# Mixture-of-experts FFN in a two-layer macaron block: every expert for every token, or tiles of routed rows

## The chip, the core and the metric

The kernel runs on one core of a Trainium2 chip. The metric is the device time of one execution in microseconds. Three runs of the kernel before gave 2809.14, 2815.56 and 2818.88 us.

## The reference

The input is 16 sequences of 256 tokens with 128 features, 4096 tokens in fp32. There are two layers; each is half an FFN, an attention, and half an FFN. Cut to what matters:

```python
x = x + 0.5 * ffn0(layernorm(x)); x = x + attn0(layernorm(x)); x = x + 0.5 * ffn0(layernorm(x))
x = x + 0.5 * ffn1(layernorm(x)); x = x + attn1(layernorm(x)); x = x + 0.5 * ffn1(layernorm(x))

# layer 0: one shared expert, eight routed ones, the two best by gate count; hidden width 128
probs = softmax(x @ gate_w + gate_b); topk_probs, topk_idx = top_k(probs, 2)
cw    = sum(one_hot(topk_idx, 8) * topk_probs)            # zero for six experts of eight
hr    = einsum('bsd,edf->ebsf', x, rw1) + rb1             # a, b = halves of hr
out_e = einsum('ebsf,efd->ebsd', silu(a) * b, rw2) + rb2
out   = shared(x) + einsum('ebsd,bse->bsd', out_e, cw)
# layer 1: eight experts, hidden width 256, gelu, the two weights divided by their sum + 1e-6
```

Attention has 16 heads of 8 features, with two softmaxes per head in layer 0 and one causal softmax in layer 1. The change leaves its arithmetic alone.

## The kernel before

All 4096 tokens stay in SBUF (`xs`) as 8 blocks of 512 tokens, tokens on partitions. An item is a sublayer on one block; `items` (lines 517 to 522) lists 8 blocks of FFN00, then attention 0, FFN01, FFN10, attention 1 and FFN11 (first digit the layer, second the FFN in it). An item yields units of up to three stages, and `step` runs one stage each of three successive units side by side. In the second or third unit of an item, the next item's `prepare` is written into the instruction order. Each engine's queue takes its instructions in the order of the program.

An FFN item's `prepare` normalizes the block (`normalized_T`: statistics on VectorE, a power on GpSimd at line 142, transposes on TensorE, a copy on ScalarE) and computes the gates (`gates`: logits at 165, ranks by comparing every pair of experts at 187 to 194, weights at 195 to 207). The weights per token, `cw`, are transposed, written to DRAM (`cwD`, line 214), and read back spread over all partitions, 256 KB for each expert (`load_spread`, line 263).

Each unit is one expert (in layer 1 half an expert, as its hidden width is two times 128) on all 512 tokens: two products with 512 columns (231, 232), an activation on ScalarE (234), one VectorE instruction for bias and product (236), a GpSimd multiply by the spread weights (300) that zeroes what was not routed, and the output product added in PSUM (316). A block has 9 units in layer 0 and 16 in layer 1. After the last one, `finish_ffn` transposes the sum and adds half of it to x. All expert weights lie in SBUF from the start, loaded by DMAs from ScalarE's queue.

Attention works on two sequences per block; its units cover four heads and one softmax each. VectorE's maxima (421 in layer 0, 416 in layer 1) go to `mpad`, which TensorE transposes before the second set of scores (393, tile `ss_a`).

Of the kernel before, what the change touches and what calls it, by code (L numbers as in the profile page):

```python
# [9 lines left out]
BF = mybir.dt.bfloat16  # L10
AF = mybir.ActivationFunctionType
# [4 lines left out]
P = 128  # L16
# [5 lines left out]
def kernel(ctx: ExitStack, tc: tile.TileContext, a: dict, out: bass.AP):  # L22
    """Two macaron layers (half FFN, attention, half FFN) over x [B, T, C].

    x stays in SBUF, tokens on partitions. Each sublayer works on blocks of 512 tokens (two
    sequences). Feature-major activations [C, tokens] feed the matrix products. Everything is fp32,
    except for the causal mask's constants.
    """
# [6 lines left out]
    NCH = TB // P  # token chunks of a block  # L35
    BPB = TB // T  # sequences of a block
    NBLK = B * T // TB
    NT = T // P  # token chunks of a sequence
    G = H // 4  # heads go four to a group, each in a strip of 32 partitions
# [5 lines left out]

    const = ctx.enter_context(tc.tile_pool(name="const", bufs=1))
# [3 lines left out]
    gatep = ctx.enter_context(tc.tile_pool(name="gate", bufs=2))  # L50
    ffp = ctx.enter_context(tc.tile_pool(name="ffn", bufs=3))
    atp = ctx.enter_context(tc.tile_pool(name="attn", bufs=2))
    dram = ctx.enter_context(tc.tile_pool(name="dram", bufs=2, space=bass.MemoryType.DRAM))
# [26 lines left out]
    gate_w0 = wp.tile([P, E], FP, name="gate_w0")  # L80
    nc.scalar.dma_start(out=gate_w0, in_=a["L0_ffn_gate_w"])
    gate_b0 = bcast_row(a["L0_ffn_gate_b"], E, "gate_b0")

# [5 lines left out]
    # Layer 0: expert 0 here is the shared one, the routed ones follow.  # L89
    w1_0 = [load(a["L0_ffn_sw1"][0], [P, 2 * F0], "sw1")]  # L90
    w2_0 = [load(a["L0_ffn_sw2"][0], [P, C], "sw2")]
    for e in range(E):
        w1_0.append(load(a["L0_ffn_rw1"][e], [P, 2 * F0], f"rw1_{e}"))
        w2_0.append(load(a["L0_ffn_rw2"][e], [P, C], f"rw2_{e}"))
    # The output biases, a row per expert and the shared one's last.
    b2_0 = wp.tile([E + 1, C], FP, name="b2_0")
    nc.scalar.dma_start(out=b2_0[0:E, :], in_=a["L0_ffn_rb2"])
    nc.scalar.dma_start(out=b2_0[E : E + 1, :], in_=a["L0_ffn_sb2"])

    # Hidden biases with features on partitions: load rows, transpose.  # L100
    def hidden_bias(parts, name):
        rows = sum(p.shape[0] for p in parts)
        raw = wp.tile([rows, P], FP, name=name + "_raw")
        r = 0
        for p in parts:
            nc.scalar.dma_start(out=raw[r : r + p.shape[0], :], in_=p)
            r += p.shape[0]
        ps = small(name + "_ps")
        nc.tensor.transpose(ps[:, :rows], raw, ident[:rows, :rows])
        t = wp.tile([P, rows], FP, name=name)  # L110
        nc.vector.tensor_copy(t, ps[:, :rows])
        return t

    b1_0 = hidden_bias(
        [
            a["L0_ffn_sb1"].rearrange("e (k f) -> (e k) f", f=P),
            a["L0_ffn_rb1"].rearrange("e (k f) -> (e k) f", f=P),
        ],
        "b1_0",
    )  # L120

# [1 line left out]
    mhalf = const.tile([P, NCH], FP, name="mhalf")  # L123
    nc.gpsimd.memset(mhalf, -0.5)
    # earlier[e, f] = 1 where f < e: of equal gates, the lower index goes first.
# [7 lines left out]
    def normalized(src, nchunk, dst, key):  # L133
        """dst = (src - mean) / sqrt(var + eps) over the last axis, chunk by chunk."""
# [13 lines left out]
    def normalized_T(n, key):  # L148
        """The block's layernorm with features on partitions, [C, 512]."""
        xn = lnp.tile([P, NCH, C], FP, tag="xn", name=f"xn_{key}")  # L150
        normalized(xs[n], NCH, xn, key)
        ps = small(f"xnT_ps_{key}")
        for c in range(NCH):
            nc.tensor.transpose(ps[:, c * P : (c + 1) * P], xn[:, c, :], ident)
        xnT = lnp.tile([P, TB], FP, tag="xnT", bufs=3, name=f"xnT_{key}")
        nc.scalar.copy(xnT, ps)
        return xnT

    def gates(xnT, gate_w, gate_b, layer, key):
        """The experts' weights for the block's tokens, [E (+ 1), 512] with a row of ones for the  # L160
        shared expert: in SBUF, and in DRAM, from where rows are spread over the partitions."""
        rows = E + 1 if layer == 0 else E
        ps = small(f"lg_ps_{key}")
        for c in range(NCH):
            nc.tensor.matmul(
                ps[:, c * E : (c + 1) * E], lhsT=xnT[:, c * P : (c + 1) * P], rhs=gate_w,
                start=True, stop=True,
            )
        lg = gatep.tile([P, NCH, E], FP, tag="lg", name=f"lg_{key}")
        nc.vector.tensor_tensor(  # L170
            lg, ps[:, : NCH * E].rearrange("p (c e) -> p c e", e=E),
            gate_b.unsqueeze(1).to_broadcast([P, NCH, E]), ALU.add,
        )
        mx = gatep.tile([P, NCH, 1], FP, tag="mx", name=f"mx_{key}")
        nc.vector.tensor_reduce(mx, lg, AX.X, ALU.max)
        ex = gatep.tile([P, NCH, E], FP, tag="ex", name=f"ex_{key}")
        nc.vector.tensor_tensor(ex, lg, mx.to_broadcast([P, NCH, E]), ALU.subtract)
        nc.scalar.activation(ex, ex, AF.Exp)
        sm = gatep.tile([P, NCH, 1], FP, tag="sm", name=f"sm_{key}")
        nc.vector.tensor_reduce(sm, ex, AX.X, ALU.add)  # L180
        nc.vector.reciprocal(sm, sm)
        # rank = how many experts go before this one; the first two are taken.
        other = lg.unsqueeze(2).to_broadcast([P, NCH, E, E])
        own = lg.unsqueeze(3).to_broadcast([P, NCH, E, E])
        gt = gatep.tile([P, NCH, E, E], FP, tag="gt", name=f"gt_{key}")
        eq = gatep.tile([P, NCH, E, E], FP, tag="eq", name=f"eq_{key}")
        nc.vector.tensor_tensor(gt, other, own, ALU.is_gt)
        nc.vector.tensor_tensor(eq, other, own, ALU.is_equal)
        nc.gpsimd.tensor_tensor(
            eq, eq, earlier.unsqueeze(1).to_broadcast([P, NCH, E, E]), ALU.mult  # L190
        )
        nc.vector.tensor_tensor(gt, gt, eq, ALU.add)
        rank = gatep.tile([P, NCH, E], FP, tag="rank", name=f"rank_{key}")
        nc.vector.tensor_reduce(rank, gt, AX.X, ALU.add)
        nc.vector.scalar_tensor_tensor(ex, rank, 1.5, ex, ALU.is_lt, ALU.mult)
        cw = gatep.tile([P, NCH, E + 1], FP, tag="cw", name=f"cw_{key}")
        nc.vector.tensor_tensor(cw[:, :, 0:E], ex, sm.to_broadcast([P, NCH, E]), ALU.mult)
        if layer == 0:
            nc.gpsimd.memset(cw[:, :, E : E + 1], 1.0)
        else:  # L200
            top = gatep.tile([P, NCH, 1], FP, tag="top", name=f"top_{key}")
            nc.vector.tensor_reduce(top, cw[:, :, 0:E], AX.X, ALU.add)
            nc.vector.tensor_scalar(top, top, 1e-6, None, ALU.add)
            nc.vector.reciprocal(top, top)
            nc.vector.tensor_tensor(
                cw[:, :, 0:E], cw[:, :, 0:E], top.to_broadcast([P, NCH, E]), ALU.mult
            )
        psT = small(f"cwT_ps_{key}")
        for c in range(NCH):
            nc.tensor.transpose(psT[:rows, c * P : (c + 1) * P], cw[:, c, 0:rows], ident)  # L210
        cwT = gatep.tile([E + 1, TB], FP, tag="cwT", bufs=3, name=f"cwT_{key}")
        nc.scalar.copy(cwT[:rows], psT[:rows])
        kept = dram.tile([E + 1, TB], FP, tag="cw", bufs=3, name=f"cwD_{key}")
        nc.sync.dma_start(out=kept[:rows], in_=cwT[:rows])
        return cwT, kept

    def finish_ffn(n, acc, key):
        """x += 0.5 * acc^T"""
        oT = ffp.tile([P, TB], FP, tag="oT", bufs=2, name=f"oT_{key}")
        nc.scalar.copy(oT, acc)  # L220
        ps = small(f"o_ps_{key}")
        for c in range(NCH):
            nc.tensor.transpose(ps[:, c * P : (c + 1) * P], oT[:, c * P : (c + 1) * P], ident)
        nc.vector.scalar_tensor_tensor(
            xs[n].rearrange("p c d -> p (c d)"), ps, 0.5, xs[n].rearrange("p c d -> p (c d)"),
            ALU.mult, ALU.add,
        )
# [17 lines left out]
    class FFN:  # L245
        def __init__(self, layer, which, n, last=False):
            self.layer, self.n, self.last = layer, n, last
            self.key = f"f{layer}{which}_{n}"
# [375 lines left out]
    while under_way:  # L624
        step()
# [33 lines left out]
```

## Time and profile before

| | us |
|---|---|
| median of three runs (lowest to highest) | 2815.56 (2809.14 to 2818.88) |
| profiled execution, its span from the first to the last instruction | 2803.8 |
| busy TensorE, VectorE, ScalarE, GpSimd in it | 2554.9, 1174.8, 1010.8, 625.8 |
| FFN00, 36 to 262 | 226 |
| attention 0, 262 to 1305 | 1043 |
| FFN01 and FFN10, 1305 to 1855 | 550 |
| attention 1, 1855 to 2440 | 585 |
| FFN11, 2440 to 2803 | 363 |

PE is TensorE's matrix products, PEld its weight loads, DVE VectorE, ACT ScalarE, POOL GpSimd, SP SyncE. Names that end in q stand for an engine's own queue. A line such as "L300 POOL TENSOR_TENSOR hw_f<-h_f,cwb_f ... x384 | 485.4, 1266 | 644.8 <-DVE h_f" gives source line, engine, operation, tile written and tiles read, count, busy time in us, the mean of one in ns, the time the engine idled before such instructions, and what ended that idling. A row of windows gives the window and its length, each engine's busy time with its count of instructions, the granted clock of TensorE as a share of full speed, the share of the DMA engines' time, and GB/s. An fp32 product has two records for each pass in the timeline ("x2").

### The profile page before, as it was taken

To read this page: it belongs to the slowest core of one execution; us is meant where nothing else is said; L and a number is where in the kernel's file an instruction comes from. 1 tells how busy PE (TensorE), PEld (TensorE's weight loads), DVE (VectorE), ACT (ScalarE), POOL (GpSimd) and SP (SyncE) were. 2 spreads that over 40 slices of the span, in tenths; PEclk is the share of its full clock that TensorE was granted. 3 is DMA by queue.
4 is the path that set the end of the run, shared out by engine and by line. 5 is a ranking of instruction groups with operands and counts; after the bars stand their busy time and mean duration, and the time that the engine had idled before them with its cause. 6 is when DMAs were issued, how large, how long until landed. Compare 5 with 4: busy or idle time off the path is not lost.

```text
span 2803.8 us, 36494 instructions
## 1 busy us (share of the span) xinstructions
PE 2554.9 (91%) x14660; PEld 1376.0 (49%) x14660; DVE 1174.8 (42%) x2553; ACT 1010.8 (36%) x1525; POOL 625.8 (22%) x595
## 2 busy tenths in 40 slices
PE   4999888888888888887999999999999999999999
PEld 2444555555555555553444444445555555544443
DVE  4443444444444444445444343434443444434332
ACT  1333434333334333344334333323333333333332
POOL 3443000000000010002444444440000000144444
PEclk8999989999989888899999999999999999999999
DMA  5221000000000000000121102110000000021110
GB/s 143 79 74 59 1 1 1 1 1 1 1 1 1 1 1 1 1 20 31 61 91 61 61 31 61 37 35 1 1 1 1 1 1 1 20 65 42 60 56 32
DMA packets 63968, 79.90 MB, mean 28 GB/s; under 512 B 16355, under 2 KB 29734, under 8 KB 63798
## 3 DMA queue, kind: packets, MB, share of 16 engines
q1 hardware_dynamic: 45856, 71.88, 7.8%
q10 hardware_dynamic: 17942, 5.69, 0.9%
q8 instruction: 115, 1.88, 0.3%
q14 instruction: 55, 0.45, 0.1%
HBM read 74.89 MB, written 2.65 MB: 28 GB/s over the span
## 4 chain that ended last, share of the span: by engine, by line
PE 79%; DVE 13%; DMA 2%; POOL 2%; issue 2%; ACT 1%; ACTq 0%; SPq 0%; POOLq 0%; DVEq 0%
PE sm_a L393 12%; PE acc_f L316 10%; PE hid_f L231 10%; PE ss_a L393 9%; PE hid_f L232 9%; PE av_a L454 8%; DVE mpad L421 6%; PE pq_a L376 3%; PE pq_a L377 3%; PE po_a L468 2%; PE pm_a L432 2%; PE ss_a L387 2%; DMA cwb_f<-cwD_f 2%; PE sm_a L387 1%; PE acc_f L309 1%
## 5 line engine op out<-in xcount | busy, mean ns | idle before, releaser
L300 POOL TENSOR_TENSOR hw_f<-h_f,cwb_f 128x512 f32<-128x512 f32 x384 | 485.4, 1266 | 644.8 <-DVE h_f L236 586.3
L441 ACT ACTIVATE ex_a<-ss_a 128x1024 f32<-128x1024 f32 (+1 forms) x384 | 365.4, 952 | 588.0 <-PE ss_a L393 587.9
L393 PE MATMUL ss_a<-q_a,k_a 32*128 32x256 f32 (+1 forms) x3072 | 426.0, 397 | 151.7 <-DVE mpad L421 146.3
L236 DVE SCALAR_TENSOR_TENSOR h_f<-hid_f,b,s_f 128x512 f32<-128x512 f32 x384 | 287.9, 750 | 572.3 <-ACT s_f L234 571.4
L234 ACT ACTIVATE s_f<-hid_f,b 128x512 f32<-128x512 f32 x384 | 263.8, 687 | 622.7 <-PE hid_f L232 622.2
L421 DVE TENSOR_REDUCE mpad<-sm_a 128x4 f32<-128x1024 f32 x256 | 313.6, 1225 | 403.5 <-PE sm_a L393 307.0
L393 PE MATMUL sm_a<-k_a,q_a 32*128 32x256 f32 (+1 forms) x3072 | 429.5, 398 | 0.5 <-ACT k_a L379 0.5
L393 PEld LDWEIGHTS ss_a<-q_a,k_a 32*128 32x128 f32 x3072 | 272.2, 192 | 264.4 <-DVE mpad L421 198.8
L393 PEld LDWEIGHTS sm_a<-k_a,q_a 32*128 32x128 f32 x3072 | 253.7, 193 | 142.7 <-issue 90.7
L454 PE MATMUL av_a<-ex_a,vaug 128*32 128x256 f32 (+1 forms) x3072 | 266.8, 385 | 0.0
L316 PE MATMUL acc_f<-hw_f,W 128*128 128x512 f32 x512 | 263.1, 596 | 1.3 <-POOL hw_f L300 1.3
L232 PE MATMUL hid_f<-xnT_f,W 128*128 128x512 f32 x512 | 262.8, 595 | 0.0
L231 PE MATMUL hid_f<-xnT_f,W 128*128 128x512 f32 x512 | 261.7, 593 | 0.7 <-ACT ex_a L441 0.7
L490 POOL TENSOR_TENSOR o_a<-pr_a 128x256 f32<-128x256 f32 x16 | 11.6, 724 | 876.6 <-DVE pr_a L487 876.6
L416 DVE TENSOR_REDUCE mpad<-sm_a 128x2 f32<-128x256 f32 (+1 forms) x256 | 131.0, 554 | 109.9 <-PE sm_a L393 109.3
L316 PEld LDWEIGHTS acc_f<-hw_f,W 128*128 128x128 f32 x512 | 95.7, 190 | 127.2 <-issue 123.8
L454 PEld LDWEIGHTS av_a<-ex_a,vaug 128*32 128x32 f32 x3072 | 96.7, 112 | 116.1 <-issue 58.3
L231 PEld LDWEIGHTS hid_f<-xnT_f,W 128*128 128x128 f32 x512 | 95.8, 190 | 114.4 <-issue 107.1
L232 PEld LDWEIGHTS hid_f<-xnT_f,W 128*128 128x128 f32 x512 | 94.0, 190 | 102.2 <-issue 101.8
L464 ACT COPY avs_a<-av_a 128x512 f32<-128x512 f32 (+1 forms) x128 | 61.3, 479 | 218.4 <-PE av_a L454 218.4
L316 PE MATMUL acc_f<-hw_f,rw 128*128 128x512 f32 x256 | 132.5, 599 | 6.9 <-POOL hw_f L300 6.7
L231 PE MATMUL hid_f<-xnT_f,rw 128*128 128x512 f32 x256 | 133.1, 602 | 2.6 <-ACT ex_a L441 2.0
(132 smaller groups left out, 2464.1 us busy)
## 6 DMA issues: line engine op xcount, KB each, us to landing
cwb_f<-cwD_f SPq DMA_DIRECT2D x256, 256.0 KB
x<-in_L_attn_x_dram SPq DMA_DIRECT2D x8, 256.0 KB
W<-in_L_ffn_W_dram ACTq DMA_DIRECT2D x8, 256.0 KB
out_dram<-x SPq DMA_DIRECT2D x8, 256.0 KB
rw<-in_L_ffn_rw_dram ACTq DMA_DIRECT2D x8, 128.0 KB
W<-in_L_ffn_W_dram ACTq DMA_DIRECT2D x8, 128.0 KB
rw<-in_L_ffn_rw_dram ACTq DMA_DIRECT2D x8, 64.0 KB
cwD_f<-cwT_f SPq DMA_DIRECT2D x16, 18.0 KB
```

The lines of the kernel that those rows point to most:

```text
L231: nc.tensor.matmul(hidden[:, 0, :], lhsT=lhs_act, rhs=xnT, start=True, stop=True)
L232: nc.tensor.matmul(hidden[:, 1, :], lhsT=lhs_lin, rhs=xnT, start=True, stop=True)
L234: nc.scalar.activation(s, hidden[:, 0, :], func, bias=bias_act)
L236: nc.vector.scalar_tensor_tensor(h, hidden[:, 1, :], bias_lin, s, ALU.add, ALU.mult)
L300: nc.gpsimd.tensor_tensor(hw, h, self.spread[e], ALU.mult)
L316: nc.tensor.matmul(self.acc, lhsT=w2, rhs=made["h"], start=False, stop=last)
L376: nc.tensor.matmul(pq[:, 0:T], lhsT=wq[:, w, g, :], rhs=seq["x"], start=True, stop=True)
L393: nc.tensor.matmul(sc[:, jj, col : col + size], lhsT=stationary[s, w, c * P : (c + 1) * P], rhs=moving[s, w, first : first + size], start= ...
L416: nc.vector.tensor_reduce(mp[:, c, 2 * jp : 2 * jp + 2, D : D + 1], sc[:, :, col : col + size], AX.X, ALU.max, negate=True,)
L421: nc.vector.tensor_reduce(mp[:, :, 2 * jp : 2 * jp + 2, D].rearrange("p c j -> p j c"), sc.rearrange("p j (c s) -> p j c s", s=T), AX.X, A ...
L441: nc.scalar.activation(ex[:, 2 * jp : 2 * jp + 2, :], sc[:, :, : self.cols], AF.Exp, scale=ATT_SCALE)
L454: nc.tensor.matmul(av[32 * j : 32 * j + 32, w * T + first : w * T + first + size], lhsT=seq["v"][:, c, 4 * g + j, :], rhs=u["ex"][:, j, co ...
```

## The change

The tokens are taken in halves of four blocks (2048 tokens), and each FFN computes only the rows that were routed.

- At the start the experts' weights, output bias (repeated on 128 rows) and hidden bias are copied into one DRAM table per layer (`wcat`, by `gather_weights`), and two DRAM buffers for rows (`slots_x`, 5888 rows each) are filled with zeros. All of these DMAs are issued from ScalarE's queue.
- `dispatch` normalizes four blocks, computes the gates, ranks, counts and start positions for the whole half, and so each token's two slots (`idx`), its two weights (`wgt`) and each tile's expert (`rows`). Then 32 indirect DMAs on GpSimd's queue scatter the normalized rows, 128 rows of 512 bytes each, to slots in DRAM. Each expert's rows start at a multiple of 256.
- `units` first runs, in layer 0, the shared expert on the four blocks, and then 23 tiles of 256 rows. For each tile SyncE reads the expert's row into a register, loads that expert's weights from DRAM (263 KB in layer 0, 461 KB in layer 1, four buffers) and the tile's rows. TensorE transposes the rows, computes the hidden products (two or four with 256 columns) and the output products (two or four with 128 columns), VectorE adds the output bias, and the rows are written to DRAM (`slots_y`) from ScalarE's queue.
- `combine` gathers the two rows of each token back with 32 indirect DMAs of 128 rows on GpSimd's queue; VectorE adds each, times its weight, to x.
- The order is written out by hand: `dispatch`, `combine` and the normalization for attention are generators in the list `between`, of which `advance` takes a few parts after each unit. The attention of one half is placed between FFNs of the other.
- The spread loads, the GpSimd multiply by the weights, the transposes of `cw` and of the output sum, and the weights kept in SBUF are gone.

```diff
+    def gather_weights(layer):
+        w1, w2, b2, b1 = srcs[layer]
+        wc = dram.tile([E * P, WC[layer]], FP, name=f"wcat{layer}")
+        nc.scalar.dma_start(out=wc[:, 0:col], in_=w1.rearrange("e p f -> (e p) f"))
...
+        nc.scalar.dma_start(
+            out=sx.rearrange("(p i) d -> p i d", p=P),
+            in_=zero.to_broadcast([P, NSLOT // P, C]),
+        )
...
     class FFN:
+        def dispatch(self):
...
+            nc.vector.tensor_tensor(eq, other, own, ALU.is_equal)
+            nc.gpsimd.tensor_tensor(eq, eq, earlier.unsqueeze(1).to_broadcast(s4), ALU.mult)
...
+            for c in range(HCH):
+                for j in range(2):
+                    s = nc.gpsimd.indirect_dma_start(
+                        out=self.sx[:, :],
+                        out_offset=bass.IndirectOffsetOnAxis(ap=idx[:, j, c : c + 1], axis=0),
+                        in_=self.xn[c // NCH][:, c % NCH, :], in_offset=None,
+                    )
+                yield
...
+        def load_tile(self, j):
+            wt = ffp.tile([P, WC[layer]], FP, tag="wt", bufs=4, name=f"wt_{k}")
+            row = nc.sync.value_load(self.rows[0:1, j : j + 1], min_val=0, max_val=(E - 1) * P)
+            nc.sync.dma_start(out=wt, in_=wcat[layer][bass.ds(row, P), :])
+            xg = ffp.tile([P, 2, C], FP, tag="xg", bufs=4, name=f"xg_{k}")
+            ld = nc.sync.dma_start(
+                out=xg, in_=self.sx[j * TS : (j + 1) * TS, :].rearrange("(p i) d -> p i d", i=2)
+            )
+            for s in self.scattered:
+                tc.add_manual_dep(ld.ins, s.ins.name, SYNC, reason="every row may be here")
...
+        def output(self, u):
...
+            nc.vector.tensor_tensor(
+                y, ps[:, :TS].rearrange("p (i d) -> p i d", i=2), b2, ALU.add
+            )
+            nc.scalar.dma_start(
+                out=self.sy[j * TS : (j + 1) * TS, :].rearrange("(p i) d -> p i d", i=2), in_=y
+            )
...
+        def combine(self):
+            for i, n in enumerate(self.blocks):
+                for c in range(NCH):
+                    t = i * NCH + c
+                    for j in range(2):
+                        g = ffp.tile([P, C], FP, tag="g", bufs=8, name=f"g_{self.key}_{t}_{j}")
+                        nc.gpsimd.indirect_dma_start(
+                            out=g[:, :], out_offset=None, in_=self.sy[:, :],
+                            in_offset=bass.IndirectOffsetOnAxis(
+                                ap=self.idx[:, j, t : t + 1], axis=0
+                            ),
+                        )
+                        nc.vector.scalar_tensor_tensor(
+                            xs[n][:, c, :], g, self.wgt[:, j, t : t + 1], xs[n][:, c, :],
+                            ALU.mult, ALU.add,
+                        )
+                    yield
...
+    compute(0, 0, 0, 3)
+    compute(0, 0, 1, 3)
+    attend(0, 0, 0, 4, 1)
+    attend(0, 1, 0, 2, 2)
+    compute(0, 1, 0, 2)
+    attend(0, 1, 2, 4, 2)
+    compute(1, 0, 0, 2)
+    compute(0, 1, 1, 2)
+    attend(1, 0, 0, 3, 3)
+    compute(1, 0, 1, 2)
+    attend(1, 0, 3, 4, 3)
+    attend(1, 1, 0, 4, 2)
+    compute(1, 1, 0, 3)
+    compute(1, 1, 1, 3)
```

`compute(layer, which, half, rate)` runs the units of one FFN half and `attend(layer, half, first, last, rate)` the attention of some of its blocks; `rate` is how many parts of the generators follow each unit.

## The prediction

> **What bounds the kernel now.** I read the page's first part for the busiest engine, then the table by windows, cut at the stages, then the timeline, the groups and the chain of waits for the price of one instruction. A difference of 0.3% (8.4 us) is about what a measurement of this kernel can tell from no change.
>
> ```profile
> PE 2554.9 (91%) x14660; PEld 1376.0 (49%) x14660; DVE 1174.8 (42%) x2553; ACT 1010.8 (36%) x1525; POOL 625.8 (22%) x595
> PE 79%; DVE 13%; DMA 2%; POOL 2%; issue 2%; ACT 1%; ACTq 0%; SPq 0%; POOLq 0%; DVEq 0%
> ```
> TensorE is busy 91% and carries 79% of the chain that ended last. The windows are: start, FFN00, attention 0, FFN01 with FFN10, attention 1, FFN11 (columns: length, busy time of PE, PEld, DVE, ACT, POOL; granted clock, DMA share, GB/s).
>
> ```profile
> 0.00:36.00 36.00, 8.74 (x25) 5.04 (x25) 17.61 (x83) 2.67 (x4) 15.73 (x41) 1.00 0.63 143
> 36.00:262.00 226.00, 207.12 (x570) 93.07 (x571) 91.91 (x220) 80.59 (x114) 87.89 (x82) 0.96 0.26 87
> 262.00:1305.00 1043.00, 886.24 (x7326) 545.65 (x7324) 455.05 (x741) 411.04 (x599) 70.04 (x93) 0.91 0.01 2
> 1305.00:1855.00 550.00, 530.07 (x1428) 237.19 (x1428) 241.28 (x637) 194.70 (x275) 255.32 (x220) 1.00 0.18 60
> 1855.00:2440.00 585.00, 567.31 (x4387) 336.16 (x4386) 232.65 (x592) 202.51 (x366) 27.86 (x25) 0.99 0.01 3
> 2440.00:2803.00 363.00, 355.40 (x928) 158.89 (x926) 136.36 (x283) 119.27 (x171) 168.95 (x137) 1.00 0.15 49
> ```
> The FFN stages are bound by PE (530 of 550 us): 226 + 550 + 363 = 1139 us can shrink. The two attentions, 1628 us, are not changed in their own work. The timeline of a steady FFN stretch gives the price of a product: starts 0.86 us apart for 512 fp32 columns, so 0.43 for 256.
>
> ```profile
> 1600.15 1.02 PE L316 MATMUL acc_f<-hw_f,W 128*128 128x512 f32 x2
> 1601.01 1.02 PE L231 MATMUL hid_f<-xnT_f,W 128*128 128x512 f32 x2
> 1601.87 1.02 PE L232 MATMUL hid_f<-xnT_f,W 128*128 128x512 f32 x2
> ```
> Other prices are from the groups, and the landing of a 256 KB load (4.73) and of a small write to DRAM (1.77) from the chain of waits at 1304 to 1340 us:
>
> ```profile
> L300 POOL TENSOR_TENSOR hw_f<-h_f,cwb_f 128x512 f32<-128x512 f32 x384 | 485.4, 1266 | 644.8 <-DVE h_f L236 586.3
> L236 DVE SCALAR_TENSOR_TENSOR h_f<-hid_f,b,s_f 128x512 f32<-128x512 f32 x384 | 287.9, 750 | 572.3 <-ACT s_f L234 571.4
> L435 DVE TENSOR_TENSOR q_a<-pm_a,q_a 128x256 f32<-128x256 f32 x192 | 80.1, 417 | 74.4 <-PE pm_a L432 74.4
> L379 ACT ACTIVATE k_a<-pq_a,k_ones 128x256 f32<-128x256 f32 x192 | 92.1, 480 | 0.0
> ```
> ```profile
> 1320.84 1.77 DMA cwD_f<-cwT_f
> 1324.02 4.73 DMA cwb_f<-cwD_f
> ```
>
> **What goes.** Per block, 9 units (layer 0) or 16 (layer 1) of three 512-column products: 16 blocks x 9 + 16 x 16 = 400 units, 400 x 3 x 0.86 = 1032 us of PE. With them go 384 POOL multiplies and 256 spread loads of 256 KB; both were hidden behind PE, so their going buys nothing by itself.
>
> **What comes, on PE.** Each FFN half runs 23 tiles of 256 rows whatever the routing (16 would hold 4096 chosen rows, 7 are for padding), 92 tiles per layer. A layer 0 tile: two transposes of 0.135, two 256-column products of 0.43, two 128-column ones of 0.225 = 1.58 us; layer 1: 0.27 + 4 x 0.43 + 4 x 0.225 = 2.89. That is 92 x 4.47 = 411 us, with 16 shared units of 2.62 (two 512-column, four 128-column) 453 us in all, instead of some 1100.
>
> **A tile's real period.** PE will not be the bound: the weights come from DRAM per tile into 4 buffers, and tile j+4's load can go only when tile j's last DVE instruction has read its bias. The circle for layer 0: issue 0.38 (the median of the spread load's issue), landing 4.73, hidden 0.86, ACT 0.48, DVE 0.42, output 0.45, DVE 0.42 = 7.7, and about two other tiles' PE work queued ahead, 3.2: 10.9 / 4 = 2.7 us. Layer 1: landing 5.9 (4.73 and 0.34 MB more at the 280 GB/s of the window 36:44 below), hidden 1.72, two ACT 0.96, DVE 0.42, output 0.9, DVE 0.42, issue 0.38 = 10.7, with two tiles' 5.8 16.5 / 4 = 4.1. Bytes: 525 and 723 KB a tile, at 280 GB/s 1.9 and 2.6 us, just under. Ends: 2.0 and 3.1 (bytes and PE) below; above, PE at half clock, which this trace shows where PE has idled:
>
> ```profile
> 36.00:44.00 8.00, 0.00 (x0) 0.00 (x0) 0.00 (x0) 0.00 (x0) 0.00 (x0) 0.72 0.88 280
> 44.00:52.00 8.00, 2.10 (x5) 1.03 (x5) 0.47 (x3) 2.12 (x3) 0.58 (x2) 0.50 0.69 218
> ```
> At half clock a tile's PE work is 3.2 and 5.8. I take 2.7 and 4.1, as PE would be busy 58 to 70%, nearer to attention 0 (85% busy, clock 0.91) than to a stop.
>
> **Scatters and gathers.** 32 scatters and 32 gathers of 128 rows per half, on POOL's queue, 16 phases. No indirect DMA is in the trace. Below: a plain issue of 128 rows, 0.38 us. Above: a small DRAM transfer that nothing overlaps, 1.77, or 2.3 with the next issue and a hand-over. The nearest row is a POOL instruction over all partitions, 1.27; I take 1.3, 42 us a phase. On the path: the first scatters (the first tile's load waits for all of them), the first gathers (their 32 DVE additions stand between tiles 0 and 4 of the second half, so DVE waits and later outputs behind them), the second half's gathers at the start of attention 0 (32 additions within four units, ahead of the maxima that PE waits for), and the last gathers. The other twelve lie beside tiles or attention; what they cost is in the stalls of steps 4 to 7.
>
> A rule of the Trainium skill, "DMA: Bandwidth & Descriptors", section "Anatomy of one DMA — SWDGE (gpsimd) path", fits such DMAs as 2.0 us and bytes over 436 GB/s. By it a 64 KB piece would be an estimate of 2.15 us and, if they ran one at a time, the total would come out near 2880, slower than now.
>
> DVE and POOL also get in each other's way here: the 128x32 instruction L195 takes 155 ns at best and 845 at worst.
>
> ```profile
> L195 DVE SCALAR_TENSOR_TENSOR ex_f<-rank_f,ex_f x32: 155/580/845, 32.8 to 2722.3; 128x32 f32<-128x32 f32 x32
> ```
> The Trainium skill ("SBUF — State Buffer", section "SBUF: two separate sides") speaks against this change in the same place: a DMA that GpSimd issues cannot get its descriptors written while DVE holds the port they share, and it gives 620 ns alone against 3100 beside a copy. At that price 32 pieces would be an estimate of 99 us and the change a loss; the trace before has no such DMA.
>
> **The sum by stages.**
> 1. Start. Weights copied DRAM to DRAM (2.1 and 3.7 MB, read and written), 6 MB of zeros and x: about 20 MB at 280 GB/s, 70 us; ACT's queue issues 33 of these ahead of its first copy, so its first xnT waits (PE, DVE and POOL also have waits on late loads in front). Then gates 10, routing 18 (three 1024-column DVE instructions of some 1.7, POOL's multiply 2.5, rank 1.6, about thirty of 0.2 and hand-overs), scatters 42, load 6: first tile at 146.
> 2. First half 23 x 2.7 = 62, and 10 where SP reads row numbers of the next half before loads of the fifth tile on: 218.
> 3. Second half: shared units 10.5, 62, gathers' stall 30 (42 less the four tiles beside them): 321. Before, 262.
> 4. Attention 0: 1043 + 30 (gathers in front) + 40 (two halves' routing and additions on DVE, whose maxima bound PE there already): 1434.
> 5. FFN01 and FFN10: shared 21, 46 x 2.7 = 124, 46 x 4.1 = 189, stalls 30: 1798. That is 364 against 550.
> 6. Attention 1: 585 + 55, as in 4: 2438.
> 7. FFN11: 189, stalls 30, the last 32 gathers uncovered 42, additions and output 5: 2704. That is 266 against 363.
> The sum stands against the profiled execution's span, 2803.8: 100 us less. The median of the runs lies 11.8 above that span; so 2716 us.
>
> **Rivals.**
> A. The indirect DMAs pace the kernel, 2.3 us each. One more us apiece costs 32 on each of the four exposed phases (128) and on half of four partly covered ones (64), about 190: 2906, slower. For it: DVE waits in order for each gather. Against it: the program lets eight be under way at once. It decides from 1.85 us on ((2815 - 2716) / 190 = 0.53 over 1.3).
> B. The tiles run at the half-clock ends, 3.2 and 5.8: 92 x 0.5 + 92 x 1.7 = 202 more, 2918, slower. It decides from 0.54 us more per tile. Against: a PE that becomes full gets its clock back.
> C. All is hidden: tiles 2.0 and 3.1 (92 x 1.7 = 156 less), pieces 0.8 (95 less): 2465.
> That less is computed than said cannot be: the tile count is fixed.
>
> **How the numbers follow.** The forecast, 2600 to 2807, 0.48; C 0.12; A 0.18; B 0.18; between forecast and loss, within 0.3%, 0.04. Faster 0.60, same 0.04, slower 0.36. The range takes in C's end nearly and A's and B's: 2480 to 2930; its own range for the likeliest case is 2600 to 2807.
>
> **What would show it.** The first tile's transposes near 146 us; tiles 2.7 and 4.1 us apart in compute stretches, with PE waiting on the weight's DMA; POOL's indirect DMAs 1.3 us apart; DVE waits on gathers of about 30 us at the start of the second half and in front of attention 0; 42 us of gathers after the last tile. Attention stages longer by over 100 us, or indirect DMAs over 1.85 us, would make it wrong; so would a clock near 0.5 in the tile stretches.

## The result, and the profile after

The changed kernel took 3078.07 us (median of four, 3071.83 to 3086.34), the kernel before on the same chip 2812.35: a ratio of 1.0954 (1.0925 to 1.0983). The forecast was 2716, a gain, with a range up to 2930, so its sign was wrong. The same code, run again on a later occasion (label a1_again), took 2805.77 us (median of ten, 2791.95 to 2824.06) against 2811.11, a ratio of 0.9991 (0.9966 to 1.0015). Both belong to the result: 272 us of the loss come and go with a condition of the chip that the experiments describe, and some 90 us by which the forecast was too low stay in either.

The page, busy time and shares of the chain: the first occasion, then the same code run again.

```profile
PE 2101.9 (68%) x14757; PEld 1417.9 (46%) x14757; DVE 1136.4 (37%) x2802; ACT 828.4 (27%) x1467; POOL 654.2 (21%) x706
PE 51%; DVE 12%; another core or an unknown queue 10%; issue 9%; DMA 8%; POOL 5%; ACT 2%; ACTq 1%; SPq 1%; POOLq 0%; DVEq 0%
```
```profile
PE 2084.3 (75%) x14757; PEld 1404.3 (50%) x14757; DVE 1139.3 (41%) x2802; ACT 829.2 (30%) x1467; POOL 653.4 (23%) x706
PE 53%; DVE 13%; DMA 12%; POOL 9%; issue 9%; ACT 1%; ACTq 1%; SPq 1%; POOLq 0%; DVEq 0%
```
TensorE has 2102 us of work, not 2555, and no longer bounds the kernel: it is busy 68%. "Another core or an unknown queue" holds 10% of the first chain, on a kernel with one core; in the second it is gone. Both groups of indirect DMAs cost about what was forecast, 0.95 us and 0.30 between two, so 1.26 each and 40 us for 32, which I call a train:

```profile
L534 POOL DMA_INDIRECT g_f<-slots_y,idx_f x256 | 243.0, 949 | 647.6 <-DMA slots_y<-y_f 227.8
L400 POOL DMA_INDIRECT slots_x<-xn_f,idx_f x256 | 246.5, 963 | 203.7 <-DVE high_f L381 79.4
```
What the others do meanwhile is the finding. Windows of the first occasion, undisturbed attention and then the scatter train at 1004.8 (length, PE, PEld, DVE, ACT, POOL, clock, DMA share, GB/s):

```profile
500.00:540.00 40.00, 34.48 (x308) 22.11 (x310) 15.26 (x19) 17.45 (x26) 0.00 (x0) 0.97 0.01 1
1005.00:1045.00 40.00, 7.06 (x60) 3.68 (x52) 3.14 (x5) 2.63 (x3) 30.55 (x32) 0.59 0.24 78
```
TensorE does 7 us of work in 40 instead of 34, and VectorE and ScalarE do not fill the gap. The chain in that train (start, length, what):

```profile
1009.89 2.11 PE sm_a L622 x8
1012.00 0.03 issue
1012.02 0.02 DVEq L664
1012.04 0.04 issue
1012.09 0.43 DVE q_a L664
1012.51 37.53 another core or an unknown queue
1050.05 0.02 issue
1050.07 1.24 DVE mpad L650
```
The maxima at 1050.07 wait for TensorE alone, by their semaphore; TensorE's last product before them ended at 1014.65. The timeline shows the same on ScalarE, whose copy also waits only for the product above it:

```profile
1008.22 1.67 PE L683 MATMUL av_a<-ex_a,vaug 128*32 128x256 f32 x16
...
1034.64 0.58 ACT L693 COPY avs_a<-av_a 128x512 f32<-128x512 f32 x1 [25.86 <-remote]
```
The product ended at 1009.89, the copy began 24.8 us later. The trace also records each raise of the counter (the semaphore) by which the others learn that a product has ended. The raise itself comes late: five of TensorE's products here ended at 1007.92, 1008.29, 1009.89, 1010.95 and 1014.64, the raises on record are at 1010.57, 1012.00, 1034.62, 1050.05 and 1050.14, and the copy and the maxima begin 0.02 us after the third and the fourth. Outside trains a raise comes 0.02 us after the end of its product on average; inside them about 5 us, 42.8 at worst, some 870 us over 174 raises (each end taken with the next raise on record; 31 of 2210 raises are missing from the record, so single values may be too high). The waits of the whole run that end on such a late raise ("remote") do not depend on this matching. They sum to 690 us on VectorE and ScalarE, often side by side; the kernel before and a1_again have none. The longest of them (us in total, times, longest):

```profile
ACT avs_a L693 <- remote: 142.3, 6, 38.1
DVE mpad L645 <- remote: 94.0, 6, 35.6
DVE mpad L650 <- remote: 76.8, 3, 37.6
```
I call this the hold-up. By stages, in us of span:

| | forecast | first occasion | run again | p6_both (below) |
|---|---|---|---|---|
| start and FFN00 | 321 | 392 | 348 | 343 |
| attention 0 | 1113 | 1292 | 1219 | 1116 |
| FFN01, FFN10 | 364 | 360 | 316 | 317 |
| attention 1 | 640 | 766 | 681 | 636 |
| FFN11 | 266 | 263 | 226 | 231 |
| sum | 2704 | 3073 | 2790 | 2643 |

The stages are cut at VectorE's first and last addition of the output bias (L516) in an FFN half. So what lies between attention's last product and the first finished tile, some of the shared expert's units among it, counts as attention. Cut at attention's last product on TensorE instead, the two attentions are 1245 and 734 us on the first occasion, 1172 and 649 run again, and 1084 and 617 in p6_both.

### The profile page after: what moved, and what is told of

Read it like the earlier page. It is cut to its first block, busy times and chain, and to the rows that moved or that the text cites. A ratio compares the mean times of both kernels' runs of the same rounds, so it can differ in the third digit from the quotient of the medians.

```text
span 3072.5 us, 38949 instructions
## 1 busy us (share of the span) xinstructions
PE 2101.9 (68%) x14757; PEld 1417.9 (46%) x14757; DVE 1136.4 (37%) x2802; ACT 828.4 (27%) x1467; POOL 654.2 (21%) x706
## 4 chain that ended last, share of the span: by engine, by line
PE 51%; DVE 12%; another core or an unknown queue 10%; issue 9%; DMA 8%; POOL 5%; ACT 2%; ACTq 1%; SPq 1%; POOLq 0%; DVEq 0%
PE sm_a L622 10%; PE ss_a L622 8%; PE av_a L683 7%; PE hid_f L484 6%; DVE mpad L650 5%; DMA wt_f<-wcat 5%; PE pq_a L605 3%; PE pq_a L606 3%; PE po_a L697 2%; PE pm_a L661 2%; POOL g_f L534 2%; PE ss_a L616 2%; PE y_ps_f L510 2%; DMA xg_f<-slots_x 2%
## 5 line engine op out<-in xcount | busy, mean ns | idle before, releaser
L484 PE MATMUL hid_f<-xT_f,wt_f 128*128 128x256 f32 x1104 | 309.5, 425 | 130.4 <-DMA wt_f<-wcat 71.9
L534 POOL DMA_INDIRECT g_f<-slots_y,idx_f x256 | 243.0, 949 | 647.6 <-DMA slots_y<-y_f 227.8
L484 PEld LDWEIGHTS hid_f<-xT_f,wt_f 128*128 128x128 f32 x1104 | 218.1, 210 | 185.9 <-DMA wt_f<-wcat 73.2
L400 POOL DMA_INDIRECT slots_x<-xn_f,idx_f x256 | 246.5, 963 | 203.7 <-DVE high_f L381 79.4
L492 ACT ACTIVATE s_f<-hid_f,wt_f 128x256 f32<-128x256 f32 x276 | 120.9, 471 | 385.5 <-PE hid_f L484 234.0
L497 DVE SCALAR_TENSOR_TENSOR h_f<-hid_f,wt_f,s_f 128x256 f32<-128x256 f32 x276 | 125.3, 478 | 249.7 <-ACT s_f L492 193.7
L510 PE MATMUL y_ps_f<-wt_f,h_f 128*128 128x128 f32 x1104 | 174.1, 292 | 63.5 <-ACT xT_f L473 26.6
L510 PEld LDWEIGHTS y_ps_f<-wt_f,h_f 128*128 128x128 f32 x1104 | 160.2, 205 | 82.3 <-ACT xT_f L473 27.7
L721 POOL TENSOR_TENSOR o_a<-pr_a 128x256 f32<-128x256 f32 x16 | 11.6, 722 | 860.9 <-DVE pr_a L718 860.9
L605 PE MATMUL pq_a<-xnT_a,wq 128*128 128x256 f32 x384 | 145.8, 469 | 0.0
L516 DVE TENSOR_TENSOR y_f<-y_ps_f,wt_f 128x256 f32<-128x256 f32 x184 | 75.9, 420 | 181.5 <-PE y_ps_f L510 90.5
```

The source lines that it names most:

```text
L400: s = nc.gpsimd.indirect_dma_start(out=self.sx[:, :], out_offset=bass.IndirectOffsetOnAxis(ap=idx[:, j, c : c + 1], axis=0), in_=self.xn[c ...
L484: nc.tensor.matmul(hid[:, z, k * TS : (k + 1) * TS], lhsT=wt[:, (base + k) * P : (base + k + 1) * P], rhs=xT, start=True, stop=True,)
L497: nc.vector.scalar_tensor_tensor(h[:, k, :], hid[:, 1, k * TS : (k + 1) * TS], wt[:, bias + lin0 + k : bias + lin0 + k + 1], s[:, k, :], A ...
L510: nc.tensor.matmul(ps[:, i * P : (i + 1) * P], lhsT=u["h"][:, k, i * P : (i + 1) * P], rhs=wt[:, w2 + k * C : w2 + (k + 1) * C], start=(k ...
L534: nc.gpsimd.indirect_dma_start(out=g[:, :], out_offset=None, in_=self.sy[:, :], in_offset=bass.IndirectOffsetOnAxis(ap=self.idx[:, j, t : ...
L605: nc.tensor.matmul(pq[:, 0:T], lhsT=wq[:, w, g, :], rhs=seq["x"], start=True, stop=True)
```

## The experiments

Theory 1: trains of indirect DMAs hold up TensorE's hand-overs. Theory 2: the program's own waits for gathers and staged rows cost the time. Theories 3 and 4 came later.

**Trains added to the kernel before.** Each of these adds 256 DMAs of 64 KB whose data nobody reads, meant for attention 0.

m1_train asks for eight groups of 32, m2_spread for two per unit:

```diff
+    def extra(n):
+        for _ in range(n):
+            g = ffp.tile([P, C], FP, tag="g", bufs=8, name=f"g_{turn['g']}")
+            nc.gpsimd.indirect_dma_start(out=g[:, :], out_offset=None, in_=x_rows,
+                in_offset=bass.IndirectOffsetOnAxis(ap=rowi[:, 0:1], axis=0))
...
+            if NBLK <= i < 2 * NBLK and j == 4:
+                extra(32)      # m2_spread: extra(2) in every unit
```


> The kernel before, with 8 trains of 32 indirect gathers (128 rows of x, 64 KB each) on GpSimd's queue, one train per block of attention 0; nothing reads what they bring. Theory 1 (a train of indirect DMAs holds up the other engines' semaphore updates until it ends, as the gaps of 18 to 46 us in the trace after suggest): each train freezes attention for about 30 of its 40 us, so 8 x 30 = 240 us more, about 3050, and the same gaps in the semaphore updates. Theory 2 (the time after is lost in waits of the program: DVE's additions, the tile loads and the row buffers wait for the data): nobody waits for these, so within 10 us of before.

> The same 256 unread gathers, two after each of the 128 units of attention 0 instead of in trains. GpSimd's queue has nothing else to wait for, so it may still run them in trains early; if they do come out evenly, theory 1 expects a loss in proportion to the time in which one is under way (256 x 1.26 = 320 us at the most, 100 to 250 if hand-overs slip between). Theory 2: within 10 us of before.

3011.72 and 3014.97 us (2807.76 before; 1.072 and 1.073). Nothing ties the gathers to their units, so GpSimd ran all of them ahead, from 19 to 400 us in both kernels, and FFN00's multiplies (L300) queued behind them: TensorE's products wait 126 us for them in m1_train, 7.9 in the kernel before. That is a loss by GpSimd's order, which says nothing of the theories. TensorE's raises were 0.01 us late. I passed over that then; it counts below.

m3_plain has plain DMAs of the same size from GpSimd's queue instead (0.54 us each).

> The trains of m1_train with plain DMAs of the same 64 KB from GpSimd's queue in place of indirect ones. If the hold-up belongs to any DMA that GpSimd writes descriptors for, the loss is like m1_train's per DMA; if it belongs to the indirect ones alone, it is under 20 us. Theory 2: within 10 us of before.

2863.99 us (1.0195). GpSimd ran these ahead too, from 19 to 243 us, and TensorE's products wait 28 us for the multiplies.

m4_train ties each train to a unit of attention 0 by row numbers that VectorE makes from that unit's maxima:

```diff
+        nc.vector.scalar_tensor_tensor(
+            idx, mp[:, 0, 0, D : D + 1], 0.0, rowf, ALU.mult, ALU.add)
+        for _ in range(32 if turn["u"] % 16 == 4 else 0):   # m7_pairs: range(2)
+            g = ffp.tile([P, C], FP, tag="g", bufs=8, name=f"g_{turn['g']}")   # m5_train2: 2
+            nc.gpsimd.indirect_dma_start(...)               # m6_plain: dma_start, to DRAM
```


> The kernel before with 8 trains of 32 unread indirect gathers, this time tied to attention 0: the row numbers come from a small DVE instruction in each of its 128 units (0.17 us, about 20 us in all at the most), and one unit in 16 is followed by 32 gathers with 8 buffers. In m1_train GpSimd ran all 256 ahead in FFN00, in front of its multiplies, so that run does not tell the theories apart. Theory 1 (a train holds up the hand-overs between the other engines): PE does a fifth to a half of its usual work in each 40 us train, 8 x 20 to 32 = 160 to 260 us more, 2970 to 3070. Theory 2 (program waits): at most the 20 us of small instructions, under 2830.

> m4_train with 2 buffers for the gathers in place of 8, so that at most two are under way. If what holds up the others is the number of indirect DMAs under way, the loss per train falls by half or more, to under 100 us in all; if it is GpSimd's work on each of them, it stays as in m4_train, per time spent in the train. Theory 2: under 2830.

> m4_train with plain DMAs (64 KB from SBUF to DRAM) from GpSimd's queue in place of the indirect ones, 8 trains of 32. If any DMA whose descriptors GpSimd writes holds up the others, 8 x 32 x 0.54 us = 138 us of trains cost 70 to 110 us more than before; if only indirect ones do, it is at most the 20 us of small instructions. Theory 2: the same 20 us.

> m4_train's 256 gathers as pairs, two after the maxima of each of the 128 units, instead of 8 trains. If the hold-up is of the time in which an indirect DMA is being issued, whatever its neighbours, 128 pairs of 2.5 us cost as much as the trains (160 to 260 us); if a train has to build up (its first 7 to 11 us passed freely in the trace after), pairs cost under 60 us. Theory 2: under 2830.

Against 2814.06 on the same occasion: m4_train 3095.84 (1.1008), 282 us or 35 for each train that nobody reads; m5_train2, whose two buffers put its gathers 1.37 us apart, 3010.59 (1.0705), 25 for each train, between its two expectations; m6_plain 2843.82 (1.0112); m7_pairs 2806.27 (0.9991, 0.9968 to 1.0015). The windows of m4_train, its first train and then no train, and of m7_pairs:

```profile
292.00:332.00 40.00, 11.41 (x86) 7.03 (x78) 3.16 (x5) 4.13 (x7) 30.31 (x32) 0.63 0.18 51
400.00:440.00 40.00, 33.18 (x329) 20.33 (x328) 18.13 (x27) 16.77 (x24) 0.00 (x0) 1.00 0.00 1
```
```profile
271.00:311.00 40.00, 34.01 (x283) 21.70 (x283) 17.27 (x26) 17.11 (x25) 11.60 (x12) 0.96 0.07 20
```
The same 256 gathers cost 282 us in trains and nothing in pairs, and no engine needs their data: theory 1 for this occasion, with no help from theory 2. The waits of VectorE and ScalarE that end on a late raise sum to 499 us in m4_train, 286 in m5_train2, and none in m6_plain and m7_pairs. GpSimd's order is not the reason here: VectorE waits 13.4 us for attention's own GpSimd instructions (`o_a`, L492) in m4_train, as in the kernel before.

m8_space and m9_space_s put a GpSimd memset of 128x768 or 128x256 after each gather of m4_train, which stretches 1.25 us to 1.88 and 1.44.

> m4_train with a GpSimd memset of 128x768 (about 0.75 us) between the gathers of a train, so one every 2.0 us in place of 1.25; the same 256 gathers, trains of 64 us. Theory 1 as the runs have left it (the hold-up builds up only where indirect DMAs follow one another at GpSimd's own pace; m7_pairs cost nothing): at most the 20 us of small instructions, 2800 to 2840. If the hold-up is of any time in which GpSimd works on an indirect DMA in a long row, spaced or not: 2950 to 3100.

> m8_space with a shorter memset (128x256, 0.31 us), one gather every 1.6 us. It places the threshold: m4_train at 1.25 us a gather lost 35 us per train, m5_train2 at 1.37 lost 24. If what is saturated needs about 1.4 us per DMA, next to nothing is lost here (under 2850); if it needs 1.7 or more, over 2900.

2903.23 us (1.0336), 12 for a train, and 2943.89 (1.048), 17, on another chip and occasion. In m9_space_s 140 us of the waits of VectorE and ScalarE end on a late raise; in m8_space none does. Most of what m8_space loses comes from GpSimd's order: its trains last 60 us, attention's GpSimd instructions queue behind them, and VectorE waits 76.2 us for these instead of 13.4 (TensorE in turn 75.1 us for VectorE's `q_a` instead of 5.4):

```profile
DVE st_a L138 <- POOL o_a L492: 76.2, 16, 11.0
```
So the hold-up shrinks with the gap between indirect DMAs: 499, 286 and 140 us of such waits at 1.25, 1.37 and 1.44 us, and none at 1.88.

**The changed kernel, taken apart.** p1_paced lets each scatter read a ScalarE copy of its rows in one of four buffers, and each gather's addition come two parts later, with six buffers instead of eight:

```diff
+                stage = lnp.tile([P, C], FP, tag="stage", bufs=4, name=f"stage_{key}_{c}")
+                nc.scalar.copy(stage, self.xn[c // NCH][:, c % NCH, :])
```


> The changed kernel with its 512 indirect DMAs paced: each scatter reads a copy that ScalarE makes in the unit in which it is due (4 buffers), and each gather's buffer (6) is given back by additions that come two parts later, so at most a few indirect DMAs can run in a row. Theory 1, if a hold-up ends with each short group: 150 to 300 us faster than the changed kernel, 2780 to 2920; if only the number of indirect DMAs counts, no change (3078). Theory 2: the additions wait less for their gathers, up to 120 us faster (the 118.5 us that DVE's additions waited for gathers).

2880.4 us (1.0251), 198 less than the first occasion, and raises 2.2 us late at most. I took that for a proof that waits in GpSimd's queue cure the hold-up. Its trains say otherwise: still 32 DMAs 1.26 us apart. The last three runs took this reading down.

p2_space puts the 128x768 memset after each indirect DMA except the first 32 and the last 32.

> The changed kernel with the memset of m8_space after each indirect DMA, except in the first scatters and the last gathers, which nothing runs beside. Theory 1: the freezes of 14 trains go, 14 x 25 to 32 us less, and the trains' own length (64 us) is waited for where tiles or x wait for them, 4 x 24 us back: 2700 to 2850. Theory 2 (waits for the data): the data come later, so slower than 3078 by up to 200.

2917.19 us (1.0389), 161 less than the first occasion, between the ranges of the two theories. Both are at work: late raises end 53 us of waits, all beside the first 32 scatters, which have no memset; but the other trains now last some 60 us, and VectorE waits 285 us for gathers instead of 118.5. The spacing takes the hold-up away and pays for it in the program's waits.

p4_anchor ties each pair of row numbers to the unit being written, and adds one part later:

```diff
+            nc.vector.scalar_tensor_tensor(
+                idx, anchor["col"].to_broadcast([P, 2]), 0.0, at[:, :, c], ALU.mult, ALU.add)
...
+            anchor["col"] = h[:, 0, 0:1]            # a tile's hidden rows
...
+                anchor["col"] = mp[:, 0, 0, D : D + 1]   # attention's maxima
```


> The changed kernel, with each pair of row numbers made by a small DVE instruction that reads a column of the unit being written (a hidden tile or an attention tile), so that a scatter's or gather's two indirect DMAs go out with that unit and not in a train of 32; eight gather buffers, and a gather's addition one part later. Theory 1 (a train of indirect DMAs at GpSimd's own pace holds up the hand-overs from PE to DVE and ACT until it ends; pairs of them do not, as the 256 gathers in pairs cost nothing in the kernel before): about ten of the sixteen trains go, some 25 to 35 us each, less what the anchors and the later additions cost: 2700 to 2850, most likely near 2790, PE's updates late by under 0.3 us on average inside the remaining pairs. Theory 2 (the program's own waits for gathers and staged rows cost the time, whatever the spacing): it stays at 2950 to 3080, and DVE's waits on gathers do not shrink.

p5_plain uses plain DMAs of the same size, to and from fixed rows, with a memset of 128x640 after each:

```diff
-                    s = nc.gpsimd.indirect_dma_start(
+                    s = nc.gpsimd.dma_start(
+                        out=self.sx[k * P : (k + 1) * P, :], in_=self.xn[c // NCH][:, c % NCH, :]
...
+                        s = nc.gpsimd.dma_start(out=g[:, :], in_=self.sy[k : k + P, :])
```


> The changed kernel with its 512 indirect DMAs replaced by plain DMAs of the same size from GpSimd's queue, to and from fixed rows of the same DRAM buffers, and a GpSimd memset of 128x640 after each so that they keep a pace of about 1.25 to 1.9 us: the rows are not routed, the waits of the program stay as they are. Theory 1 (the indirect kind of DMA holds up the hand-overs): without it the forecast's sum holds for the rest, 2650 to 2800, and PE's updates come under 0.1 us late. Theory 2 (the waits for 32 paced DMAs of any kind, in their order, cost the time): 2900 to 3080, as the waits are the same.

p4_anchor 2883.3 (1.0252), above the range of theory 1; p5_plain 2666.82 (0.9492), inside it, and 411 less than the first occasion, without a late raise. Not all of the 411 is due to the kind of DMA. a1_again, with indirect DMAs and no hold-up, took 2805.77, so 139 us have another reason, and p5_plain changes more than the kind: its gathers are 1.10 us apart, and its scatters read no row numbers, so they do not wait for the ranks. The first tile's transposes come at 145 us instead of 166.5, and the scatters that a1_again sends in one train at 951 go in five groups of 4 and 8 between 459 and 895. In p4_anchor the lateness follows the length of what is left of the trains: summed over the raises inside, less than 0.3 us for a group of two, 1.6 for four, 7 for eight, 63 for sixteen, on average.

So p6_both allows one pair in each unit (two in four places), and takes the next half's rows through the layer norm only after the last half's scatters; p7_nopause drops its memsets.

```diff
+        while pair["last"] == pair["tick"] and pair["n"] >= most and under_way:
+            yield WAIT
...
+                yield from next_unit(key + "s")     # and before each pair of gathers
```


> p4_anchor taken on: not more than one pair of indirect DMAs with one unit (two in four places where an FFN needs them soon), the next half's layer norm after the last one's scatters, and between tiles a GpSimd memset of 128x256 after each indirect DMA. Only the first 32 scatters and the last 32 gathers are left as trains. Theory 1 (trains hold up the hand-overs): what p4_anchor still loses against p5_plain (2883 less 2667) is mostly in its remaining trains of 4 to 32, so it should come to 2700 to 2820, and might pass the kernel before. Theory 2 (the waits of the program): 2850 to 2950, since the pairs now come later than in p4_anchor, and tiles and norms wait for them.

> p6_both without the memsets between tiles: there a pair per tile of about 2.8 us leaves GpSimd only 0.3 us between pairs. Theory 1: the hand-overs are late again in the six FFN stretches, so it is 20 to 100 us slower than p6_both. Theory 2: the same as p6_both or a little faster, as the DMAs are issued no later.

2652.92 us (0.9457, 0.9429 to 0.9485) and 2650.56 (0.9446, 0.9412 to 0.9479): faster than both kernels, by more than either theory gave. p7_nopause is a miss, as theory 1 expected 20 to 100 us more; perhaps the tie to a tile already spaces its pairs. Late raises still end 93 us of VectorE's and ScalarE's waits in p6_both, against 690 on the first occasion. p6_both's page:

```profile
PE 2075.4 (79%) x14757; PEld 1404.0 (53%) x14757; DVE 1157.9 (44%) x3050; ACT 826.1 (31%) x1465; POOL 731.7 (28%) x930
PE 52%; DVE 15%; DMA 12%; issue 9%; POOL 6%; another core or an unknown queue 2%; ACT 1%; ACTq 1%; SPq 1%; DVEq 0%; POOLq 0%
```
**Which condition.** s1_staged has only p1_paced's staged scatters, a1_again nothing new.

> The changed kernel with one half of p1_paced: each scatter reads a ScalarE copy of its rows from one of four buffers, so a scatter waits for ScalarE and ScalarE for the fourth scatter back; the gathers stay as they are. p1_paced kept 32 indirect DMAs at 1.26 us, as the changed kernel has them, and yet had no late hand-over; so the pace alone is not what holds them up. Theory 3 (a train holds up the hand-overs only where GpSimd's queue never has to wait for a landing that another engine passes on): the eight scatter trains are clean, PE's updates under 0.1 us late in them, the gather trains are as before, and the time is near the middle of 2880 and 3078, 2950 to 3020. Theory 4 (p1_paced ran in a state of the chip in which trains do no harm): all trains are alike, clean (2850 to 2930) or late (3050 to 3100).

> The changed kernel, unchanged, beside s1_staged on the same chip. Theory 3: 3060 to 3090 as before, with PE's updates late by about 5 us on average inside the trains. Theory 4: like s1_staged, trains clean in both and 2850 to 2950, or late in both.

2920.71 us (1.0375) and 2805.77 (0.9991). Not one raise is late by 1 us in either trace, in trains of 32 at 1.26 us: theory 3 falls. Theory 4 holds: on some occasions trains cause no hold-up. The traces bear a sign of it. A DMA raises its semaphore 16 times (4096 raises for 256 gathers in m1_train); a1_again, s1_staged, p1_paced, m1_train and m2_spread hold nearly all of these raises (8153 of 8192 in a1_again), while the first occasion holds 1282, and every other run with indirect DMAs misses many too. Runs of one occasion agree in the sign, and one chip showed both on different occasions. So p1_paced and s1_staged were 75 and 115 us slower than the changed kernel in their condition, not faster: ScalarE, which copies, waits in its order for the fourth scatter back. The waits of p1_paced show it (line, what ended the wait, us in total, times, longest):

```profile
ACT stage_f L400 <- DMA slots_x<-stage_f,idx_f: 213.2, 104, 5.5
DVE x L547 <- DMA g_f<-slots_y,idx_f: 192.6, 189, 5.6
```


> p6_both, unchanged, on another occasion. The changed kernel took 3078 us on its first occasion and 2806 on a later one (a1_again), where no hand-over was late. p6_both was measured on an occasion on which some were still late (266 us of late updates in sum). If its pairs are short enough for the hold-up not to matter, it comes out within 1% of 2653 in either condition; if the late updates that it still had cost time, it is 30 to 80 us faster where the records of the DMAs' semaphores are complete (the sign of the condition without hold-up), and the same as before where they are not.

2667.44 us (0.9488, 0.9438 to 0.9539), within 1% of 2653, on an occasion whose records are again incomplete. What it takes where they are complete was not measured.

**What is left without a hold-up.** Windows of a1_again in four trains of attention 0: gathers at 351, scatters at 951, gathers at 1280, scatters at 1438.

```profile
351.00:391.00 40.00, 17.10 (x112) 10.05 (x104) 14.37 (x36) 6.18 (x9) 30.17 (x32) 0.71 0.20 51
951.00:991.00 40.00, 33.18 (x316) 20.78 (x310) 18.45 (x26) 18.43 (x27) 30.56 (x32) 1.00 0.25 79
1280.00:1320.00 40.00, 18.69 (x112) 11.13 (x112) 14.29 (x36) 6.18 (x9) 30.04 (x32) 0.66 0.20 51
1438.00:1479.00 41.00, 16.15 (x112) 9.55 (x110) 8.27 (x21) 6.18 (x9) 31.61 (x33) 0.65 0.28 95
```
The second line shows that scatters alone cost nothing: TensorE does 33 us in 40. Beside gathers it does half. The waits in 1280:1320 and in 1436:1482 name the reasons:

```profile
DVE x L540 <- DMA g_f<-slots_y,idx_f: 25.8, 23, 3.3
```
```profile
DVE st_a L218 <- POOL o_a L721: 25.6, 1, 25.6
```
VectorE meets 32 additions ahead of its next maxima and waits for nearly each gather, 1.26 us apart. And attention has GpSimd instructions of its own (L721), which queue behind a train; VectorE waits 25.6 us for one. It is not the sum of the waits for gathers that p6_both lowers: in the two attentions it is 132 us there and 100 in a1_again. But they come a pair at a time, and beside the first gathers of p6_both's attention 0 TensorE does 34 us in 40:

```profile
348.00:388.00 40.00, 34.48 (x285) 22.20 (x286) 19.09 (x36) 16.50 (x25) 10.12 (x11) 0.96 0.07 21
```

## Why the prediction was wrong, step by step

- **What goes** and **what comes on PE**: by their terms TensorE's busy time would be 2555 - 1032 + 453 = 1976 us; it is 2102, and 2084 run again. The mean granted clock was 0.824 and 0.855 instead of 0.96, which may have lengthened part of the products; how much of the 108 to 126 us that is, no run isolates.
- **Start**: the first tile's transposes, forecast near 146 us, came at 174.7 and 166.5 run again, and the first stage took 71 and 27 us more than its 321.
- **Tiles** of 2.7 and 4.1 us: in the halves that no train meets 2.76 (layer 0) and 3.63 (layer 1, 0.5 too dear) in a1_again. FFN01, FFN10 and FFN11 came out 88 us under the forecast there by the cut of the table, 10 by the other. The last gathers, forecast at 42 us, took 40.
- **Indirect DMAs** at 1.3 us: right, 1.26. The rule in the Trainium skill, "DMA: Bandwidth & Descriptors", section "Anatomy of one DMA — SWDGE (gpsimd) path", gave an estimate of 2.15 us for one. In a1_again a DMA lands 2.2 us (scatters) and 2.6 us (gathers, medians) after its issue, yet the next one starts at 1.26. Read as a landing time the figure is near; as a pace it is not.
- **VectorE against descriptors** (the Trainium skill, "SBUF — State Buffer", section "SBUF: two separate sides"): the page's stall of a GpSimd DMA beside VectorE is not seen; the longest scatter (L400) took 1.23 us on the first occasion and 1.32 in a1_again. The harm went the other way.
- **The step that failed** is "The other twelve lie beside tiles or attention; what they cost is in the stalls of steps 4 to 7", with its terms of 30 and 40 in attention 0 and 55 in attention 1. Against the kernel before, attention took 249 and 181 us longer on the first occasion, 176 and 96 in a1_again. So 430 us, and 272 run again, stand in place of the 125 forecast (351 and 193 by the other cut). Two things make up the difference. First, in either condition, the order of the program: p6_both, which spreads the additions and the indirect DMAs over the units, brings attention to 1116 and 636, near the forecast's 1113 and 640. It joins several edits, and no run tells what each of them gives; p5_plain, with gathers still in trains of 32, lies between a1_again and it, at 1183 and 649. The forecast priced "32 additions within four units" as 30 us once, and did not ask for attention's GpSimd instructions behind a train at all, though it named POOL's queue. Second, in the first condition only, the hold-up, 283 us of span over all stages, a term that the sum does not have; nothing in the trace of before could have shown it, since that has no indirect DMA.
- **Rivals.** A had the right waiter (VectorE in order) at the wrong price: with 1.26 us its deciding point of 1.85 (1.3 + 0.52 is 1.82) is not reached, and VectorE's order cost without it. B is seen as an effect: the clock falls to 0.59 to 0.71 in trains where TensorE starves, and is 1.00 in the scatter train at 951. C is out.
- "Attention stages longer by over 100 us" was named as what would make the forecast wrong. It did.

Not settled: what makes the condition, and how a train delays another engine's raise. Every time on record comes with a span and a granted clock, so all are of recorded executions; as late raises and missing records come together, the recording itself may have a part in the hold-up, and no run tells. m6_plain and p5_plain show that the plain kind, from the same queue, with as many bytes and at 0.54 and 1.10 us, does not; that the two went along with held-up runs is the evidence that they met the same condition.

## What to carry to other kernels

Don't price a string of DMAs by its issuing engine alone: ask which in-order queue meets its results next, and spread issue and use over the units, a pair at a time, with a data tie that keeps the issuing engine from running ahead. A generator that takes few parts per unit does not do that by itself, as m2_spread and the changed kernel show. And before a difference is put down to an edit, run the unedited kernel beside it: here the code's own time differed by 272 us between occasions, while the kernel before stayed within 0.3%.

## What the runs showed of the hardware that I had not expected

- In these recorded executions, indirect DMAs issued back to back from GpSimd went along with raises of TensorE's semaphore up to 42.8 us late; on two occasions, with the same pace of 1.26 us, they did not. Spaced 1.88 us apart, on an occasion with the hold-up (m8_space), no wait ended on a late raise.
- On the first occasion most raises of the DMAs' own semaphores are missing from the trace (1282 of 8192 are there), in a1_again almost none (8153). Late raises ended waits only in runs with many of them missing.
- SyncE's instruction after a register load (L453, SEQ_ASSERT, 0.02 us in the median) took up to 1.40 us on the first occasion, and at most 0.03 run again.
